# Pairwise bilinear products on one core: all transfers behind the head issued from GpSimd's queue

## The chip, the core and the metric

The kernel runs on one core of a Trainium2 chip. A core has a matrix engine (TensorE, PE in the profile), a vector engine (VectorE, DVE), ScalarE (ACT), GpSimd (POOL) and SyncE (SP); data moves between the chip's main memory (here "dram") and the core's on-chip memory of 128 partitions through 16 DMA engines. Any of SyncE, ScalarE and GpSimd can issue a transfer from its queue. The metric is device time in microseconds (us), the median of several executions.

## The reference

For a batch of 4096 samples with 32 fields of 64 numbers, every field is multiplied by one 64 x 64 matrix, and then each pair of fields i < j gives the elementwise product of field i and the multiplied field j: 496 pairs of 64 numbers for each sample.

```python
def reference(r_x, L0_rec_W):          # x: 4096 x 32 x 64, W: 64 x 64, float32
    vid = jnp.einsum('bfd,de->bfe', x, W)
    idx_i, idx_j = jnp.triu_indices(32, k=1)
    return x[:, idx_i, :] * vid[:, idx_j, :]      # 4096 x 496 x 64
```

The input has 33.6 MB, the output 520.1 MB.

## The kernel before

The batch lies along the free dimension: two halves of the batch times the 64 numbers of a field fill the 128 partitions, and a tile `t` holds 128 samples of each half. There are 16 tiles (`NT`), each of 32 fields. On-chip, `mem` has 445 units of 128 float32 (512 bytes) in every partition; one unit holds one field or one pair of one tile.

For each tile TensorE multiplies the 32 fields by the matrix (`half`, line 319, eight matmuls of 4 fields in a PE loop) into the accumulators `vid`, which hold one tile. VectorE then makes the tile's 496 pairs with some 17 `tensor_tensor` products (line 299): one operand from `mem` (the tile's fields), one from `vid`, the result into `mem` again. `by_block` and `products` say which pairs one product makes.

The pairs leave in 74 stores. The table `SLOTS` gives for each store the number of units and the place in `mem` where they are collected (`home`); a row of `SLOTS` is one transfer of 128 partition rows, and each row of it is one run of up to 64 KB on both sides. A place in `mem` is used again and again: a product waits until every earlier store that reads its units has landed (`after`), and a store waits until VectorE has made its units (semaphore `made`). The input comes in two blocks (`GROUPS`): tiles 0 to 7 at the start and tiles 8 to 15 in the middle, each in three pieces (`load`), tile 0 ahead of all in two transfers of its own (the head is these two and the three pieces of the first block).

The order of the transfers is that of the program: a queue issues its transfers one after another, and each issue waits for its semaphores before those behind it come to their turn. The class `Queue` keeps what each engine has waited for already, and leaves out waits that follow from others. The first store behind each block of loads also waits for the block's last piece but one (`hold`). All loads and the stores of slots 0 to 45 go through SyncE's queue, the stores from slot 46 (`SECOND`) through ScalarE's. At the end SyncE waits for all transfers. GpSimd does nothing but set four constants. The program reserves 512 bytes of each partition for GpSimd's descriptors (`dynamic_dma_scratch_size=512`), before and after.

Of the kernel before, what the change touches and what calls it, by code (L numbers as in the profile page):

```python
# [38 lines left out]
]  # L39

SECOND = 46


PAD = 24
# [111 lines left out]
def place_of(t, fields):  # L158

    first = max(begin for begin, _ in GROUPS if begin <= t)  # L160
    return TOP - (t - first + 1) * fields


def ends(tiles):
    return [begin for begin, _ in GROUPS[1:]] + [tiles]


def overlap(a, b):
    return a[0] < b[1] and b[0] < a[1]


def pairwise_bilinear_kernel(nc, x0, x, out):
# [8 lines left out]
    mem = ctx.enter_context(nc.sbuf_tensor([P, UNITS, C], F32))  # L181
# [5 lines left out]
    there = nc.alloc_semaphore("there")  # L187

    behind = {}
    sp, act, dve = (Queue(engine, behind) for engine in (nc.sync, nc.scalar, nc.vector))  # L190
    moved = []
    worked = []

    def transfer(out_, in_, units, reads, needs, queue=sp):
        sem = nc.alloc_semaphore(f"moved{len(moved)}")
        queue.issue(lambda: queue.engine.dma_start(out=out_, in_=in_), needs).then_inc(sem, 16)  # L196
        queue.note(sem, 16)
        moved.append((units, reads, sem))
        return sem

    def after(units):

        needs = [(s, 16) for u, reads, s in moved if reads and overlap(u, units)]
        last = max((n for spans, n in worked if any(overlap(units, s) for s in spans)), default=0)
        return needs + [(made, last)] * (last > 0)
# [33 lines left out]
    def load(g):  # L239
        (begin, pieces), end = GROUPS[g], ends(NT)[g]  # L240
        begin = max(begin, 1)
        low = place_of(end - 1, F)
        sems = []
        for lo, hi in pieces:
            at = (begin - 1) * F + lo - low
            sems.append(transfer(mem[:, lo:hi, :], x[:, at : at + hi - lo, :], (lo, hi), False, after((lo, hi))))
            loads.append((range(begin, end), (lo, hi), sems[-1]))
        return sems

    def loaded(t):  # L250
        units = (place_of(t, F), place_of(t, F) + F)
        return [(sem, 16) for tiles, piece, sem in loads if t in tiles and overlap(piece, units)]

    hold = load(0)
    begins = [begin for begin, _ in GROUPS]
    held = []

    def store(slot, last):
        nonlocal hold
        begin, end = STARTS[slot : slot + 2]  # L260
        home = SLOTS[slot][1]
        units = (home, home + end - begin)
        needs = [(made, last)]
        if hold:
            needs.append((hold[-2], 16))
            hold = []
        rows = out[BLOCKS[slot] : BLOCKS[slot + 1], :].rearrange("(p u) c -> p u c", p=P)
        transfer(rows[:, : end - begin, :], mem[:, units[0] : units[1], :], units, True, needs, act if slot >= SECOND else sp)


    for t in range(NT):
        if t in begins[1:]:
            hold = load(begins.index(t))
            for late in held:
                store(*late)
            held = []
        xs = (place_of(t, F), place_of(t, F) + F)
        blocks = list(products(by_block(), t * NP))
        for k, (at, n, nest, i, j) in enumerate(blocks):
            slot = bisect_right(STARTS, at) - 1  # L280
            begin, end = STARTS[slot], STARTS[slot + 1]
            home = SLOTS[slot][1]
            units = (home + at - begin, home + at - begin + n)
# [11 lines left out]
            needs = [(there, 2 * t + 2 - high), *after(units)]  # L295
# [9 lines left out]
            if at == end:  # L305
                late = (slot, counts[made])
                group = sum(behind <= slot for behind in STRETCHES)
                if t < begins[group]:
                    held.append(late)
                else:  # L310
                    store(*late)
# [65 lines left out]
```

## Time and profile before

| | |
|---|---|
| median of 3 runs | 1285.41 us (1284.17 to 1285.61) |
| span of the profiled execution, first to last instruction | 1282.6 us |
| median less that span | 2.8 us |
| VectorE busy | 1079.9 us, 84%, 273 instructions |
| TensorE busy | 179.4 us, 14%, 256 matmuls |
| data moved | 553.70 MB, 432 GB/s over the span |
| DMA packets | 11810 |

A profile is of one execution. Its own device time beside the span is not among the figures, so the 2.8 us hold what lies around the span and what differs between executions. "L299" is line 299 of the kernel. In the rows of instructions the columns are line, engine, operation, what is written and read, count, then busy time and mean duration. "SPq" and "ACTq" are the queues of SyncE and ScalarE. A transfer's time "to landing" runs from its issue to the last count of its semaphore, so it includes the time that it stands behind the transfers ahead of it.

### The profile page before, as it was taken

The page shows a single profiled execution, that of the slowest core. Times are in us where ns is not written, and L with a number is a line of the kernel's source. Part 1 is how long each engine was busy: PE and PEld are TensorE (multiplying, and loading weights), DVE is VectorE, ACT ScalarE, POOL GpSimd, SP SyncE. Part 2 cuts the span into 40 slices and gives each one's busy share as a digit, 9 for nine tenths or more (in the row PEclk, how much of TensorE's full clock was granted, in tenths as well). Part 3 has the DMA queues.
Part 4 walks back from the last instruction along what each step waited for, and adds up shares of the span by engine and source line. Part 5 has one row for each costly group of instructions (what it writes and reads, how often), then busy time and mean ns, then how long its engine had stood idle before and what let it go on. Part 6 is the DMA issues. An engine that isn't in the chain of part 4 may idle for free. (4 is left out here: it accounts for less than half of the span.)

```text
span 1282.6 us, 1255 instructions
## 1 busy us (share of the span) xinstructions
PE 179.4 (14%) x256; PEld 70.2 (5%) x256; DVE 1079.9 (84%) x273; POOL 0.2 (0%) x4
## 2 busy tenths in 40 slices
PE   2011120301111030300020111103020020201100
PEld 1000000100000010100010000001010010100000
DVE  6589989988897989998027989989988899899980
POOL 0000000000000000000000000000000000000000
PEclk8566565756656565655565655656556575656555
DMA  9999999999999999999999999999999999999999
GB/s 404 423 435 435 438 433 433 439 435 425 435 444 429 425 437 442 428 425 446 416 426 437 426 433 436 438 434 434 439 431 442 421 437 435 427 446 429 434 425 409
DMA packets 11810, 553.70 MB, mean 432 GB/s; under 512 B 1312, under 2 KB 1312, under 8 KB 1312
## 3 DMA queue, kind: packets, MB, share of 16 engines
q1 hardware_dynamic: 7776, 340.30, 61.5%
q10 hardware_dynamic: 4032, 213.39, 38.4%
q14 instruction: 2, 0.02, 0.0%
HBM read 33.59 MB, written 520.09 MB: 432 GB/s over the span
## 5 line engine op out<-in xcount | busy, mean ns | idle before, releaser
L299 DVE TENSOR_TENSOR mem<-mem,vid 128x1024 f32<-128x1024 f32 (+11 forms) x270 | 1079.3, 4065 | 161.2 <-DMA out_dram<-mem 114.5
L319 PE MATMUL vid<-mem,w 128*128 x256 | 179.4, 866 | 1016.1 <-PEq L317 1016.1
L319 PEld LDWEIGHTS vid<-mem,w 128*128 128x128 f32 x256 | 70.2, 288 | 1124.4 <-issue 1124.4
L230 DVE COPY w<-mem 64x64 f32<-64x64 f32 x2 | 0.4, 191 | 5.1 <-DMA mem<-in_r_x_dram 5.0
L227 DVE MEMSET w<- 128x128 f32 x1 | 0.2, 165 | 0.8 <-PEq L344 0.8
L344 POOL MEMSET const-bfloat16-1.0<- 128x1 bf16 x1 | 0.1, 101 | 0.0
L344 POOL MEMSET const-uint8-127<- 128x1 uint8 x1 | 0.1, 101 | 0.0
L344 POOL MEMSET const-float32-0.0<- 128x1 f32 x1 | 0.1, 98 | 0.2 <-issue 0.2
L344 POOL MEMSET const-float32-1.0<- 128x1 f32 x1 | 0.1, 98 | 0.0
## 6 DMA issues: line engine op xcount, KB each, us to landing
out_dram<-mem ACTq DMA_DIRECT2D x9, 7680.0 KB, 23.3
out_dram<-mem SPq DMA_DIRECT2D x4, 6656.0 KB, 20.5
out_dram<-mem SPq DMA_DIRECT2D x3, 7680.0 KB, 23.1
out_dram<-mem ACTq DMA_DIRECT2D x3, 7168.0 KB, 21.5
out_dram<-mem SPq DMA_DIRECT2D x5, 4096.0 KB, 17.5
out_dram<-mem SPq DMA_DIRECT2D x3, 5632.0 KB, 18.4
out_dram<-mem SPq DMA_DIRECT2D x3, 5120.0 KB, 17.3
out_dram<-mem SPq DMA_DIRECT2D x2, 7168.0 KB, 22.6
```

The costliest lines, as they stand in the source:

```text
L227: work(lambda: nc.vector.memset(w2[:, :], 0.0), [], [], made)
L230: lambda: nc.vector.tensor_copy(w2[half, half], mem[half, place + F, :D]),
L299: lambda: nc.vector.tensor_tensor(o, left, right, ALU.mult),
L319: last = nc.tensor.matmul(vid[:, b : b + BANK, :], lhsT=w2[:, :], rhs=xt(b), start=True, stop=True)
L344: nc = _bacc.Bacc("TRN2", target_bir_lowering=False, num_devices=1, dynamic_dma_scratch_size=512)
```

## The change

The three loads of the second block and all 74 stores are issued from GpSimd's queue. For such a transfer GpSimd's software writes the descriptors, the entries that tell the DMA engines what to move, and decides how they are grouped into packets; for SyncE's and ScalarE's transfers hardware does so. The five transfers of the head stay on SyncE, and the semaphores and their counts are the same.

```diff
-SECOND = 46
...
-    sp, act, dve = (Queue(engine, behind) for engine in (nc.sync, nc.scalar, nc.vector))
+    sp, pool, dve = (Queue(engine, behind) for engine in (nc.sync, nc.gpsimd, nc.vector))
...
-            sems.append(transfer(mem[:, lo:hi, :], x[:, at : at + hi - lo, :], (lo, hi), False, after((lo, hi))))
+            queue = pool if g else sp
+            sems.append(transfer(mem[:, lo:hi, :], x[:, at : at + hi - lo, :], (lo, hi), False, after((lo, hi)), queue))
...
-        transfer(rows[:, : end - begin, :], mem[:, units[0] : units[1], :], units, True, needs, act if slot >= SECOND else sp)
+        transfer(rows[:, : end - begin, :], mem[:, units[0] : units[1], :], units, True, needs, pool)
```

Before, SyncE's queue around the second block of loads, in the middle of the program (`in_r_x_dram` is the input, `out_dram` the output, the sizes are partitions x elements; `moved` are the transfers' own semaphores):

```order
L196 DMA out_dram<-mem 128x16384 [waits made] x6
L196 DMA mem<-in_r_x_dram 128x13056 [waits moved40,moved39]
L196 DMA mem<-in_r_x_dram 128x16384
L196 DMA mem<-in_r_x_dram 128x3328 [waits made]
L196 DMA out_dram<-mem 128x13312 [waits moved43,made]
L196 DMA out_dram<-mem 128x10880 [waits made]
L196 DMA out_dram<-mem 128x6528 [waits made]
L196 DMA out_dram<-mem 128x8192 [waits made]
L196 DMA out_dram<-mem 128x11264 [waits made]
L196 DMA out_dram<-mem 128x13312 [waits made]
```

After, GpSimd's queue at the same place:

```order
L192 DMA out_dram<-mem 128x16384 [waits made] x6
L192 DMA mem<-in_r_x_dram 128x13056 [waits moved40,moved39]
L192 DMA mem<-in_r_x_dram 128x16384
L192 DMA mem<-in_r_x_dram 128x3328 [waits made]
L192 DMA out_dram<-mem 128x13312 [waits moved43,made]
L192 DMA out_dram<-mem 128x10880 [waits made]
L192 DMA out_dram<-mem 128x6528 [waits made]
L192 DMA out_dram<-mem 128x8192 [waits made]
```

The sequence, the sizes and the waits are the same; only the queue is another. Before, ScalarE's queue in the second half, after it had waited from the program's start for its first store:

```order
L196 DMA out_dram<-mem 128x8192 [waits made]
L196 DMA out_dram<-mem 128x10240 [waits made]
L196 DMA out_dram<-mem 128x16384 [waits made] x4
L196 DMA out_dram<-mem 128x15360 [waits made] x2
L196 DMA out_dram<-mem 128x12288 [waits made]
L196 DMA out_dram<-mem 128x14336 [waits made]
L196 DMA out_dram<-mem 128x15360 [waits made] x2
L196 DMA out_dram<-mem 128x16384 [waits made] x5
```

These rows stand word for word in GpSimd's queue after (with the other line number), behind the last of SyncE's former stores; ScalarE's queue is empty and SyncE's holds the head's five loads. The instructions of VectorE and TensorE stand as before.

## The prediction, made before the run

> **What bounds the kernel now.** I read the page's slices first, then the DMA queues, then the stretches by window, then the waits of VectorE and of SyncE, and last the chain that ended last, which gives landing times of single transfers. The first fence is from the page: VectorE and the mean busy share of the 16 DMA engines in 40 slices of 32 us, then the packets and the queues.
>
> ```profile
> span 1282.6 us, 1255 instructions
> DVE  6589989988897989998027989989988899899980
> DMA  9999999999999999999999999999999999999999
> DMA packets 11810, 553.70 MB, mean 432 GB/s; under 512 B 1312, under 2 KB 1312, under 8 KB 1312
> q1 hardware_dynamic: 7776, 340.30, 61.5%
> q10 hardware_dynamic: 4032, 213.39, 38.4%
> ```
>
> The DMA engines stand at 9 in every slice, and the two queues' packets together fill 99.9% of the 16 engines' time. VectorE, with 84%, has holes, the DMA engines have none. The counts also tell how a transfer is cut. There are 82 transfers (46 stores and 8 loads from SyncE, 28 stores from ScalarE, below); 82 x 128 partition rows are 10496 packets, 82 x 16 engines are the 1312 packets under 512 B that signal the end, and with 2 of another queue that makes 11810. So each engine now gets 9 packets of each transfer: 8 whole rows, of up to 64 KB, and one signal. The second fence has the stores' issues, the stretches by window (the last two columns are DMA share and GB/s) and who waits on VectorE.
>
> ```profile
> L196 SPq DMA_DIRECT2D out_dram<-mem x46: 332/332/431, 38.5 to 773.7; - x46
> L196 ACTq DMA_DIRECT2D out_dram<-mem x28: 338/338/380, 785.1 to 1247.0; - x28
> L196 SPq DMA_DIRECT2D mem<-in_r_x_dram x8: 328/425/1252, 0.7 to 672.8; - x8
> 200.00:400.00 200.00, 33.13 (x48) 12.95 (x48) 188.46 (x47) 0.00 (x0) 0.60 1.01 435
> 600.00:700.00 100.00, 8.65 (x16) 3.60 (x16) 34.00 (x13) 0.00 (x0) 0.55 0.99 423
> 900.00:1100.00 200.00, 28.11 (x40) 11.01 (x40) 182.09 (x46) 0.00 (x0) 0.58 1.00 435
> DVE mem L299 <- DMA out_dram<-mem: 114.5, 35, 18.3
> DVE mem L299 <- PE vid L319: 46.5, 2, 40.7
> ```
>
> In the middle of each half the bytes go at 435 GB/s; only around the second block of loads is it 423. VectorE waits 114.5 us for stores to free their units, 35 times: it runs ahead of the transfers and is held by them. So the end is set by bytes over the transfer rate, and a change counts only if it changes that rate or leaves a DMA engine without work.
>
> **The change, part by part.** 77 transfers (74 stores, 3 loads) leave SyncE's and ScalarE's queues for GpSimd's, in the same order and with the same semaphore waits; the 5 transfers of the head stay on SyncE. No byte, no operation of VectorE or TensorE changes. The unknowns are three: how late a transfer starts behind its issue, what one row costs an engine, and whether a transfer overlaps the end of the one ahead of it. GpSimd issues no transfer in the trace of before, so each is bounded from the nearest rows. The next rows are from the chain (start, duration, what), SyncE's and ScalarE's timelines for two windows, and the transfers' groups (KB of one, us from issue to landing).
>
> ```profile
> 677.58 20.38 DMA out_dram<-mem
> 737.54 19.67 DMA out_dram<-mem
> 1002.18 23.22 DMA out_dram<-mem
> 1085.24 27.13 DMA out_dram<-mem
> 677.58 60.30 SPq L196 DMA_DIRECT2D out_dram<-mem  x6
> 1018.15 67.43 ACTq L196 DMA_DIRECT2D out_dram<-mem  x5
> out_dram<-mem SPq DMA_DIRECT2D x4, 6656.0 KB, 20.5
> out_dram<-mem ACTq DMA_DIRECT2D x9, 7680.0 KB, 23.3
> mem<-in_r_x_dram SPq DMA_DIRECT2D x1, 1056.0 KB, 5.2
> ```
>
> *The rate and the cost of a packet.* Two stretches between landings hold five stores each. The store issued at 677.58 lands at 697.96 and the one issued at 737.54 at 757.21; it is the sixth issue, so five lie in these 59.25 us. By the order of SyncE's queue they have 10880, 6528, 8192, 11264 and 13312 elements a partition: 50176 x 512 bytes are 25.69 MB. The store issued at 1002.18 lands at 1025.40, the one issued at 1085.24 at 1112.37, five issues later: 86.97 us for 12288, 14336, 15360, 15360 and 16384 elements, 37.75 MB. The difference is 12.06 MB in 27.72 us, 435.0 GB/s. At that rate the two stretches' bytes take 59.05 and 86.77 us; 0.20 us is left over in each, 0.039 us a transfer, for nine packets per engine. Each landing is read to a few hundredths; an error of 0.1 us in the 27.72 makes the rate 433.4 or 436.6 and the leftover nothing or 0.08 us.
>
> So if the software descriptors put an engine's eight rows into fewer, larger packets, at most 77 x 0.039 = 3.0 us go (6.2 us by the upper reading, nothing by the lower). If they cut rows smaller, or if fetching the descriptors costs an engine time, the cost is added; no row here shows such a fetch, and I take from once to about four times the present 0.039 us on top: 77 x 0.039 = 3.0 us to 77 x 0.16 = 12.3 us. I take the saving, since one transfer's eight equal rows on an engine lie one behind the other in one list, and every row now pays as a packet of its own; the row of 11810 packets is what it is nearest to. The Trainium skill (DMA: Bandwidth & Descriptors, section "Queues, rings and completion order") says that an engine drains a packet of typically 9 to 17 descriptors before it looks at another queue; nine is a whole share of one transfer here, and by that the 3.0 us would go nearly whole. The same page (section "SWDGE vs HWDGE vs iDMA") says that packets are preferably of at most 4096 B; by that a row of 13 to 64 KB would stay a packet of its own and the sum would be 0. No run here shows yet which holds.
>
> *The later start.* A transfer's start is hidden as long as the engines still work on the one ahead. The tightest case in the chain is the store at 737.54: it has 6656 KB, 6.82 MB, 15.7 us at 435.0 GB/s, and lands after 19.67, so it was issued 4.0 us ahead of its turn, start included. A typical one of 7680 KB, 7.86 MB, 18.1 us, lands after 23.3: 5.2 us ahead. The very first load had nothing ahead of it: 1056 KB, 1.08 MB, 2.5 us, lands 5.2 us after its issue, so a start costs at most 2.7 us from SyncE. That leaves 1.3 us or more by which GpSimd may be later than SyncE at the tightest place, 2.5 us at a typical one, at no cost. SyncE's issue takes 0.33 us; I take a GpSimd issue to cost up to a few of these more, so nothing. Where it costs more, the store is late by the excess and what is behind it on GpSimd is late with it (the third rival).
>
> *What waits on GpSimd.* The first row is the page's busy time of the engines, the second is from SyncE's waits.
>
> ```profile
> PE 179.4 (14%) x256; PEld 70.2 (5%) x256; DVE 1079.9 (84%) x273; POOL 0.2 (0%) x4
> SPq L196 <- DVE mem L299: 695.0, 44, 48.9
> ```
>
> GpSimd has no other work than four short operations. The load of the last piece in the second block and the store behind it wait for VectorE there as on SyncE, so SyncE's 695.0 us of such waits move over unchanged. In exchange ScalarE's stores, which could be issued while SyncE still held others, now stand behind them; in the trace SyncE's last issue is at 773.7 and ScalarE's first at 785.1, so they are in that order anyway: 0. The final waits stay on SyncE: 0.
>
> *The sum.* 1282.6 us of span minus 3.0 is 1279.6. The runs' median is 1285.41, 2.8 us above the profiled span, which is what lies around the span or between executions; I leave it as it is: 1285.41 - 3.0 = 1282.4 us, 0.23% faster.
>
> **The rivals.**
> First, no change: a software packet is one row, as now, or the saving is under 2.57 us. For it: rows are long, and 0.039 us in 16 is little to save. 1285.4 us.
>
> Second, slower by the rows' cost: the engines fetch descriptors that GpSimd has written to memory, and each row costs more than now. It decides from 2.57 us over 77 x 9 packets on, 3.7 ns a packet more. Doubled leftover gives 1285.4 + 3.0 = 1288.4 us, the 0.16 us of above gives 1297.7 us. Against it: a few ns are little beside the 2.4 us of a 64 KB row (65536 bytes at a sixteenth of 435.0 GB/s), and with 4 us of work queued they can be fetched ahead. For it: the engines have no idle time to hide anything in (99.9%). The Trainium skill (DMA: Bandwidth & Descriptors, "Latency and other measured facts") guesses that the engines whose memory port also serves the software descriptors' ring are slower for it; by that the slowest engines would set this rival's time, and no run here shows it yet.
>
> Third, the queue runs dry: GpSimd is later than SyncE by more than the 1.3 to 2.5 us of cover, for instance because VectorE keeps it from writing descriptors. VectorE is busy 84% of the time, and the mean of its products is the row below.
>
> ```profile
> L299 DVE TENSOR_TENSOR mem<-mem,vid 128x1024 f32<-128x1024 f32 (+11 forms) x270 | 1079.3, 4065 | 161.2 <-DMA out_dram<-mem 114.5 <-PE vid L319 46.5
> ```
>
> A store is released by the end of a product, when the next one starts; to wait that one out costs 4.1 us, of which 2.5 are covered: 1.6 us x 74 = 118 us, 1404 us. Against it: the product reads one operand from the matmul's accumulators (vid), one from mem, and nothing in the trace has GpSimd held. The Trainium skill (SBUF — State Buffer, "Who interferes with whom") has GpSimd locked out while VectorE runs in a two-port mode, and says that tensor_tensor has none; by that rule this rival does not come about.
>
> Fourth, software transfers do not overlap: each starts when the one ahead has landed. Then each pays the 2.7 us start: 77 x 2.7 = 208 us, 1493 us. Against it: the queue is still fed ahead of its turn.
>
> **How the numbers follow.** The forecast 0.41; no change 0.19; dearer rows 0.24; queue dry 0.10; no overlap 0.06. About 0.2% (2.57 us) is what a measurement of this kernel can tell from no change; its three runs lie 1.44 us apart. Faster by more than that: the forecast's 0.41. Within: 0.19. Slower: 0.24 + 0.10 + 0.06 = 0.40. The range begins at the upper reading of the saving, 1285.4 - 6.2 = 1279.2, and goes to the second rival's dear end, 1297.7; it leaves out the third and fourth rivals and 0.04 of the second. The forecast's own range is 1279.2 to 1282.8.
>
> **What would show it.** The profile after should have one software queue with 537 MB (553.70 less the head's 32832 elements x 512 bytes). Right: fewer packets or a shorter time between landings, 433.6 GB/s over such a stretch risen to 435; the DMA row 9 in all slices; a landing within 1.3 us of what it was behind its issue. Wrong: the same packet count and the same landings (first rival); the same slices at 9 but fewer GB/s (second); a slice of the DMA row under 9, and VectorE's wait for stores grown over 114.5 us (third); issue to landing of a 7680 KB store of 20.8 us with the next store's beginning only behind it (fourth).

## The result and the profile after

The changed kernel took 1291.19 us (median of 4 runs, 1289.88 to 1291.54) against 1284.79 us for the kernel before: a ratio of 1.0048, 95% interval 1.0034 to 1.0063. That is 6.4 us slower, where 3.0 us faster was forecast. The profiled span went from 1282.6 to 1289.7 us.

The page after: the span, the slices of VectorE and of the DMA engines, the packets and the queues, and GpSimd's transfers.

```profile
span 1289.7 us, 1255 instructions
DVE  6589979988897989997027989989998899899980
DMA  9999999999999999999999999999999999999999
DMA packets 11811, 553.71 MB, mean 429 GB/s; under 512 B 1312, under 2 KB 1312, under 8 KB 1312
q0 software_dynamic: 11088, 536.88, 96.7%
q1 hardware_dynamic: 720, 16.81, 3.1%
L192 POOL DMA_DIRECT2D out_dram<-mem x74 | 39.6, 536 | 1142.5 <-DVE mem L296 1142.5
```

The bytes and the packets are the same to one: 11088 is 77 x 16 x 9, so a software transfer too gives an engine eight whole rows and a signal. The DMA engines still have no empty slice. But the mean rate is 429 GB/s where it was 432: the same packets take longer. By window:

```profile
200.00:400.00 200.00, 36.82 (x48) 14.22 (x48) 187.93 (x46) 6.42 (x12) 0.57 1.00 433
600.00:700.00 100.00, 9.46 (x16) 3.90 (x16) 33.90 (x11) 3.23 (x6) 0.53 0.99 422
700.00:900.00 200.00, 36.29 (x48) 13.96 (x48) 184.65 (x55) 8.02 (x15) 0.57 1.00 428
900.00:1100.00 200.00, 29.06 (x40) 11.18 (x40) 181.16 (x47) 5.86 (x11) 0.57 1.01 434
```

The last column was 435, 423 and 435 in the first, second and fourth of these stretches (the prediction shows them); the third was, before:

```profile
700.00:900.00 200.00, 35.38 (x48) 13.77 (x48) 187.45 (x56) 0.00 (x0) 0.58 1.00 434
```

Every stretch loses a little, and the one right behind the second block of loads most, 6 GB/s. Counted by bytes, from the packets' own records in the two traces, the kernel after is 2.2 us behind when half of the bytes have moved and 3.6 us behind at 55%, around that block. In each of the other twentieths behind the first it loses 0.2 to 0.6 us, and it ends 7.1 us behind. Why more is lost around the block is not shown. The chain gives landings of the same stores as before, and VectorE's waits follow:

```profile
682.05 20.07 DMA out_dram<-mem
741.68 0.39 issue
742.08 19.29 DMA out_dram<-mem
1090.78 27.43 DMA out_dram<-mem
DVE mem L296 <- DMA out_dram<-mem: 118.0, 35, 19.1
```

Before, the issue of the store at 737.54 had this line ahead of it:

```profile
737.52 0.02 issue
```

From the landing at 702.12 (682.05 + 20.07) to that at 1118.21 (1090.78 + 27.43) there are 27 stores and 416.09 us; before it was 697.96 to 1112.37, 414.41 us. That is 1.68 us more, 0.062 us a store. The five stores up to 761.37 took 59.25 us, exactly as before, so a stretch of five is too short to read this from: a landing is that of the last of the 16 engines, while by all engines' bytes the kernel after lost 0.5 us in about the same stretch (from 55% to 60% of the bytes). Over the whole run 6.4 us are 0.083 us a transfer.

### The profile page after: what moved, and what is told of

Same layout as the page of the kernel before. It is cut to its first block, busy times and chain, and to the rows that moved or that the text cites. A ratio compares the mean times of both kernels' runs of the same rounds, so it can differ in the third digit from the quotient of the medians.

```text
span 1289.7 us, 1255 instructions
## 1 busy us (share of the span) xinstructions
PE 184.0 (14%) x256; PEld 71.6 (6%) x256; DVE 1079.9 (84%) x273; POOL 41.5 (3%) x81
## 2 busy tenths in 40 slices
DMA packets 11811, 553.71 MB, mean 429 GB/s; under 512 B 1312, under 2 KB 1312, under 8 KB 1312
## 3 DMA queue, kind: packets, MB, share of 16 engines
q0 software_dynamic: 11088, 536.88, 96.7%
## 5 line engine op out<-in xcount | busy, mean ns | idle before, releaser
L296 DVE TENSOR_TENSOR mem<-mem,vid 128x1024 f32<-128x1024 f32 (+11 forms) x270 | 1079.3, 4065 | 167.5 <-DMA out_dram<-mem 118.0
L316 PE MATMUL vid<-mem,w 128*128 x256 | 184.0, 886 | 1017.3 <-PEq L314 1017.3
L192 POOL DMA_DIRECT2D out_dram<-mem x74 | 39.6, 536 | 1142.5 <-DVE mem L296 1142.5
```

The lines of the kernel that those rows point to most:

```text
L296: lambda: nc.vector.tensor_tensor(o, left, right, ALU.mult),
L316: last = nc.tensor.matmul(vid[:, b : b + BANK, :], lhsT=w2[:, :], rhs=xt(b), start=True, stop=True)
```

## The experiments

The theory first formed from these rows (A) was the prediction's second rival: a row described by software costs an engine more. Its variant (B) puts the price on the transfer, not on the row. A rival (Q) blames the one queue.

**All on SyncE.** The kernel before with the choice of the queue taken out.

```diff
-        transfer(..., needs, act if slot >= SECOND else sp)
+        transfer(..., needs, sp)
```

> All 82 transfers from SyncE's queue, one hardware queue in one order. Theory A (a row that GpSimd's software describes costs a DMA engine more time than a row that hardware describes): as before, 1284.8 us within 0.15%. Rival Q (the loss comes from one queue in place of two, or from the one order): as after, 1291.2 us.

It took 1284.54 us beside 1284.3 for before, ratio 1.0001 (0.9992 to 1.001). One queue costs nothing; Q falls.

**Late stores alone.**

```diff
-    sp, act, dve = (Queue(engine, behind) for engine in (nc.sync, nc.scalar, nc.vector))
+    sp, pool, dve = (Queue(engine, behind) for engine in (nc.sync, nc.gpsimd, nc.vector))
...
-        transfer(..., needs, act if slot >= SECOND else sp)
+        transfer(..., needs, pool if slot >= SECOND else sp)
```

> Only the 28 late stores, ScalarE's before, go through GpSimd; the other 49 of the 77 stay on SyncE. Theory A and its variant B (the cost is once per transfer) both say 28/77 of the 6.4 us: +2.3 us, 1287.1 us. If the loss has one place (the loads in the middle, the change-over from the head) it is 1284.8 us.

1286.21 us, ratio 1.0015 (1.0006 to 1.0025): 1.9 us for 28 stores, 0.068 us each. The interval, 0.8 to 3.2 us, holds the 2.3 us of a loss in proportion. It lies above zero, so the loss is not all at the second block of loads or at the change-over from the head, which stay on SyncE here.

**Rows split, by hardware and by software.** Each row of the 77 transfers is sent as two halves, with the same number of transfers.

```diff
+        half = 2 * C * (units[1] - units[0]) if len(moved) >= 5 else 65536
-        queue.issue(lambda: queue.engine.dma_start(out=out_, in_=in_), needs).then_inc(sem, 16)
+        queue.issue(lambda: queue.engine.dma_start(out=out_, in_=in_, max_dma_last_dim=half), needs).then_inc(sem, 16)
```

> The kernel before, with each row of the 77 transfers behind the head sent as two halves: 16 rows and one signal per engine and transfer in place of 8 and one. It prices a hardware row: at the 0.039 us per nine packets of the prediction 77 x 8 x 4.3 ns = +2.7 us, 1287.5 us; at 8 ns a packet, the intercept of the packets' own durations, +4.9 us, 1289.7 us.

> The kernel after with each row of the 77 transfers as two halves, and 832 bytes per partition for the descriptors in place of 512, so that three transfers still fit. Against after (1291.2) it has the hardware split's price (2.7 to 4.9 us) in both theories. Theory A, cost per row: another 6.4 us on top, 1300 to 1302.5 us. Variant B, cost per transfer: nothing on top, 1293.9 to 1296.1 us.

By hardware 1292.26 us, by software 1300.16, beside 1284.3. The 616 more rows an engine cost hardware 8.0 us, 13 ns a row; that is three times what the prediction's two stretches gave, and above both values expected. Software costs 7.9 us over hardware with split rows, where it was 6.4 with whole ones. It should have been 12.8 by A and 6.4 by B: most of the price does not go with the rows. (The 1300.16 us itself is the number that A expected, but only because the rows cost hardware 8.0 us and not the 2.7 to 4.9 put into it.)

**Stores doubled.** Each of the 74 stores is issued as two of half the units, so rows, signals and issues double together.

```diff
...
-        queue.issue(lambda: queue.engine.dma_start(out=out_, in_=in_), needs).then_inc(sem, 16)
+        for part in (slice(0, mid), slice(mid, None)) if mid else (slice(None),):
+            queue.issue(lambda: queue.engine.dma_start(out=out_[:, part], in_=in_[:, part]), needs).then_inc(sem, 16)
...
```

The lines left out hand `mid`, half of a store's units, to `transfer`, and count 32 in place of 16 for a store; the software kernel also has the ring of 832 bytes.

> The kernel before with each of the 74 stores issued as two transfers of half the units: twice the rows, twice the signals, twice the issues, by hardware. The split rows cost 8.0 us for 616 more rows an engine, 13 ns a row; with 74 more signals at the same price about 1284.5 + 7.7 + 1.0 = 1293.2 us.

> The kernel after with the same doubling and 832 bytes for descriptors. The difference to the hardware one is the price of software descriptors for the same rows; it was 6.4 us with whole rows and 7.9 us with split rows. Theory B (once per transfer, 0.064 us, and 2.4 ns a row): about 12.5 us, 1305.7 us. Theory A (per row): 7.9 us as with split rows, 1301.1 us.

By hardware 1291.44 us, by software 1303.6, beside 1284.51. By hardware that is 1.8 us less than expected: 6.9 us for 592 rows and 74 signals more, 10 ns for each. Software costs 12.2 us over hardware, over 151 transfers 0.081 us each: the price per transfer of the plain change, with nearly the same rows as in the split pair (1208 and 1232 an engine) that cost 7.9. B, in this, is shown: twice the transfers, twice the loss.

**The ring's size.** The descriptors' memory is 832 or 256 bytes a partition in place of 512.

```diff
-    nc = _bacc.Bacc("TRN2", target_bir_lowering=False, num_devices=1, dynamic_dma_scratch_size=512)
+    nc = _bacc.Bacc("TRN2", target_bir_lowering=False, num_devices=1, dynamic_dma_scratch_size=832)
```

> The kernel after with 832 bytes for descriptors in place of 512, nothing else. If the size of the ring costs nothing (three transfers of nine entries fit in 512 bytes, the trace has at most three open): 1291.2 us. If a fuller ring makes GpSimd or the engines late: up to 6 us less, 1285 us.

> The kernel after with 256 bytes for descriptors: 16 entries an engine, so that one transfer of nine fits and the next can be described only when the one ahead has ended. This is the fourth rival made on purpose: 77 starts of up to 2.7 us, up to 208 us, 1490 us; at 2 us each 1439 us. If entries come free as soon as they are read, as after, 1291 us.

With 832 bytes it took 1291.65 us, ratio 1.0055 (1.0041 to 1.0069) to before, as after. With 256 it took 1437.86 us, 1.1193: 146.7 us over after, 1.9 us for each of 77 transfers. The page, one window, GpSimd's idle time and one group of that kernel:

```profile
span 1437.1 us, 1255 instructions
DMA  9988988998898988998888898988898988899889
q0 software_dynamic: 11088, 536.88, 86.8%
200.00:400.00 200.00, 24.57 (x32) 9.55 (x32) 165.26 (x45) 5.92 (x11) 0.55 0.90 387
L192 POOL DMA_DIRECT2D out_dram<-mem x74 | 40.0, 540 | 1314.6 <-issue 1134.8
out_dram<-mem POOLq DMA_DIRECT2D x12, 7680.0 KB, 19.8
```

This is what the fourth rival looks like: the DMA share of the window is 0.90, and a 7680 KB store that waits for nothing ahead takes 19.8 us, 1.7 more than its bytes at 435.0 GB/s. GpSimd's long idle time is put down to "issue", for which the profile shows no semaphore; a wait for room in its ring, the one thing changed, fits it. Had entries come free as soon as they are read, the time would, by the expectation, have been as after. None of that stands in the profile after, so 512 bytes keep the queue fed.

**Small loads beside the stores.** All real transfers stay on SyncE, described by hardware. With each store another queue issues a load of 16 rows of 64 bytes, one short row and one signal for each engine.

```diff
...
+        ping.issue(
+            lambda: ping.engine.dma_start(out=spare[:, :], in_=x[:16, x.shape[1] - 1, :16]),
+            [(made, last)] + [(pinged, 16 * pings)] * (pings > 0),
+        ).then_inc(pinged, 16)
...
```

`ping` is the other queue, ScalarE's or GpSimd's; the lines left out make it, the spare place and the count `pings`, and move the late stores to SyncE.

> All real transfers from SyncE; beside each of the 74 stores ScalarE issues a very small load, 16 rows of 64 bytes into a spare place, so that each DMA engine gets one short row and one signal. It prices a small hardware transfer: two packets of 9 to 13 ns, 74 x 0.02 to 0.03 us = 1.3 to 1.9 us, 1286 us.

> The same, but GpSimd issues the 74 small loads; the large transfers are all described by hardware. Theory B (a software transfer costs the engines about 0.064 us once, whatever its rows): 74 x 0.064 = 4.7 us over the same small loads from ScalarE, 1291 us. If the price goes with the number of descriptors (2 an engine in place of 9): 1.0 to 1.4 us over them, 1287.5 us. If it is the large rows themselves that run slower under software descriptors: nothing over them, 1286 us.

From ScalarE 1286.58 us, from GpSimd 1288.67, beside 1284.52. The 74 small loads cost 2.1 us by hardware, a little over the 1.3 to 1.9 expected, and 2.1 us more by software, 28 ns each. First ScalarE's kernel, then GpSimd's (packets, queues, one window):

```profile
DMA packets 14181, 553.80 MB, mean 431 GB/s; under 512 B 3681, under 2 KB 3681, under 8 KB 3681
q10 hardware_dynamic: 2368, 0.08, 0.1%
900.00:1100.00 200.00, 28.45 (x40) 11.14 (x40) 181.50 (x46) 0.00 (x0) 0.58 1.01 437
```

```profile
DMA packets 14180, 553.80 MB, mean 430 GB/s; under 512 B 3680, under 2 KB 3680, under 8 KB 3680
q0 software_dynamic: 2368, 0.08, 0.1%
900.00:1100.00 200.00, 28.69 (x40) 11.11 (x40) 181.78 (x46) 5.36 (x11) 0.57 1.00 433
```

The small packets are the same 2368 of 0.1%, yet the window falls from 437 to 433 GB/s (three other windows fall by 1 to 3). In the packets' own records a 64 KB row, described by hardware in both, takes 2423.9 ns on average beside ScalarE's small loads and 2428.0 beside GpSimd's (2423.7 in the profile before, 2431.7 after). So a software transfer is paid for also by the work in flight. The size differs from all three expectations: 28 ns is neither B's fixed 64 nor 2/9 of 83 (18).

**One packet.** The option that puts a transfer's descriptors on an engine into one packet.

```diff
-        queue.issue(lambda: queue.engine.dma_start(out=out_, in_=in_), needs).then_inc(sem, 16)
+        queue.issue(lambda: queue.engine.dma_start(out=out_, in_=in_, single_packet=queue is pool), needs).then_inc(sem, 16)
```

> The kernel after, with the option that puts all descriptors of one software transfer on an engine (eight rows and a signal) into one packet. The prediction's step, that fewer and larger packets save the rows' own overhead: up to 3.0 us less than after, 1288.2 us. Theory B (the price comes with the descriptors' arrival, whatever the packets): as after, 1291.2 us.

1291.06 us, ratio 1.0052 (1.0038 to 1.0066): as after. The option saves nothing. The profile counts 11811 packets as after, so what it counts are descriptors, and how they are grouped is not seen in it.

**What stands.** Loss of software over hardware descriptors, for one transfer, from pairs with the same rows:

| descriptors an engine and transfer | difference | transfers | each |
|---|---|---|---|
| 2 (small loads) | 2.1 us | 74 | 28 ns |
| 9 (the change) | 6.4 us | 77 | 83 ns |
| 9 (late stores alone) | 1.9 us | 28 | 68 ns |
| 9, twice the stores | 12.2 us | 151 | 81 ns |
| 17 (split rows) | 7.9 us | 77 | 103 ns |

A software transfer costs the DMA engines time of its own, which is less for 2 descriptors than for 9, but by far not in proportion. From 9 to 17 no growth is clear of noise: 7.9 us stand against 6.4, whose interval is 4.4 to 8.1. Where the engines are always busy that time is added to the end.

The kept traces show where most of it goes: into the data rows. From before to after the record of a row is 8.1 ns longer on average; with split rows it is 3.8 ns longer by software than by hardware, with doubled stores 7.6 ns. For one transfer on one engine these are 69, 62 and 62 ns, whether it has 8 rows or 16. So twice the rows bring half of the extra time for each, which is B once more. (Records of neighbouring packets can overlap a little: the DMA share of a window reaches 1.01. The shares are therefore rough.)

As far as the trace shows, GpSimd need not be writing at that moment. In the kernel with 256 bytes none of its 77 issues, of 0.54 us each, overlaps any row of its transfers, and yet the median 64 KB row takes 2424 ns, beside 2425 after and 2418 before. What the engines do in that time, reading descriptors or something else, stays open. No version tried beats the kernel before.

## Why the prediction was wrong

*What bounds the kernel* was right: the DMA engines set the end, and everything that moved the time did it through them.

*The rate and the cost of a packet* is the step that failed, in its sign. The sum took -3.0 us, 0.039 us saved for each of 77 transfers; the runs show +6.4 us, 0.083 us lost for each. The saving from "fewer, larger packets" did not come, and forcing one packet brought no more than 0.1 us. Whether the plain change grouped its rows cannot be told, since the profile counts descriptors. The cost of software descriptors stood in the same step at 3.0 to 12.3 us, but the sum left it out because no row of before showed it; that is the term that was there. The Trainium skill's two sentences on packets (DMA: Bandwidth & Descriptors, "Queues, rings and completion order" and "SWDGE vs HWDGE vs iDMA") therefore decide nothing here. The leftover of 0.039 us a transfer, read from two stretches of five stores, was also too small as the price of a row: 13 ns a row were measured, 4.3 assumed. No row was added or taken away by the change, so this did no harm to the sum.

*The second rival* came true in place, that is, the same slices at 9 with fewer GB/s, and in size: 6.4 us lie between its 3.0 and 12.3, which is why the time lies inside the whole range. That is luck in part, as these bounds were one and four times a leftover of hardware packets, which no run ties to the price of software ones. Its mechanism was told as a price per row; the runs show a price per transfer that is the same for 8 rows and for 16 within what they can tell. It had 0.24, too little beside the 0.41 of a saving that no row showed. With 77 transfers issued in another way onto engines without idle time, an unseen cost has nowhere to hide, while an unseen saving needs a mechanism.

*The later start* was right: GpSimd issues 0.39 us after VectorE's product (the row of 0.39 "issue") where SyncE took 0.02. The 6656 KB store at 742.08 lands after 19.29 in place of 19.67 us, so it is 3.6 us ahead of its turn in place of 4.0, and no slice of the DMA row shows a hole. The price of a start, at most 2.7 us as read from SyncE, came out as 1.9 from GpSimd in the 256-byte ring.

*What waits on GpSimd*: nothing was lost to the order, as the one-queue kernel shows (0.2 us). *The third rival* did not come: the 74 issues took 536 ns on average, and VectorE's products the same 4065 ns as before. VectorE's wait for stores did grow, from 114.5 to 118.0 us, but no slice of the DMA row is under 9, and slower transfers make it wait longer as well. The Trainium skill's rule (SBUF — State Buffer, "Who interferes with whom") that tensor_tensor has no two-port mode, the kind that locks GpSimd out, agrees. *The fourth* did not come either; its 208 us were 146.7 when forced.

## What to carry to other kernels

When the DMA engines are busy all the time, count transfers and rows, not issue times: here a hardware row cost 13 ns and a software transfer 0.08 us more than a hardware one, and both went straight to the end, while 0.4 us of later issue cost nothing, because the store with the least cover in the chain was still issued 3.6 us ahead of its turn. Leave large plain transfers to SyncE's and ScalarE's queues, and if GpSimd must issue them, give its ring room for several: room for three lost nothing here, and room for one cost 146.7 us, 11%. Room for two was not tried. Before forecasting a saving from something the profile does not show, ask where an equal cost could hide; on a full resource it cannot.

## What the runs showed that was not expected

Work described by hardware runs slower while software transfers are issued, though they are 0.1% of the bytes' time (the small loads, 28 ns each). And the engines do not suffer alike. Each of the 16 engines ends with one signal. In the profile after eight of these end at 1287.3 to 1287.5 us and eight at 1288.9 to 1289.4; before, ten ended at 1281.1 to 1281.4 and six at 1281.8 to 1282.2. With split rows by software eight end at 1295.8 to 1296.2 and eight at 1298.2 to 1299.0. So about 6 us fall on every engine and nearly 2 more on half of them. The second part does not grow in proportion: with the 28 late stores alone, eight end at 1283.1 to 1283.5 and eight at 1284.5 to 1285.0. The Trainium skill (DMA: Bandwidth & Descriptors, "Latency and other measured facts") guesses at some engines made slower by the descriptors' memory lying behind their port; it names two of the 16. The second part looks like it, but falls on half of the engines, and which ones they are these records do not tell.
